# A hybrid Mamba and attention block on one core: other start steps for the front and gate parts, and one convolution moved from TensorE to VectorE

## The chip, the core and the metric

The kernel runs on one core of a Trainium2 chip. A core has five engines with instruction queues of their own: TensorE (in the profile PE, its weight loads PEld), VectorE (DVE), ScalarE (ACT), GpSimd (POOL) and SyncE (SP). They meet only through semaphores. Data moves between the chip's memory and the core by DMA; here SP issues the plain transfers and POOL the accumulating ones, which add what they carry to what stands at the target. The metric is the time of one execution in microseconds, and smaller is better. A profile is one further execution, recorded by the hardware.

## The reference

The input is 8 images of 256 channels and 32 x 32 positions, taken as 8 batches of 1024 tokens, all in fp32. Layer 0 is a Mamba block and a feed-forward network; layer 1 is an attention block and a mixture of experts. Cut to what matters:

```python
# layer 0: the Mamba block
xm, z = split(layernorm(x) @ W_in)                     # 512 inner channels each
xm = silu(sum(pad(xm)[:, k:k+L] * conv_w[:, k] for k in range(4)) + conv_b)
dt, Bm, Cm = split(xm @ W_x)                           # 16 states
dt = softplus(dt @ W_dt + b_dt)
h  = exp(dt_t * A) * h + (dt_t * x_t) * B_t            # for each token t, 512 channels x 16 states
y  = sum_over_states(h * C_t) + xm * D_param
x  = x + (y * silu(z)) @ W_out
x  = x + gelu(layernorm(x) @ W1 + b1) @ W2 + b2
# layer 1
t  = t + softmax(q @ k.T / sqrt(32) + column_bias) @ v @ Wo + bo        # q, k, v of layernorm(t), 8 heads
t  = t + layernorm(xt + top-2-of-8 experts(xt))                         # xt = layernorm(t), routed per batch
```

The recurrence over the tokens has to run in their order. A batch's attention needs all its 1024 tokens, and its experts need its attention.

## The kernel before

**Chunks and steps.** The work is cut into 16 chunks of 512 tokens (`CH`). Chunk i is one half of batch i // 2: even chunks are first halves, odd ones second halves, which carry on the state of the half before. A chunk has 32 steps (`NSTEP`): 16 states for each of two halves of the 512 inner channels. A step handles one state for 256 channels, laid out as 128 partitions x 2 x 512 tokens. For each step (`now` in the main loop at the end of `hybrid_kernel`):

- `scan`: VectorE runs the recurrence over `hb` (one 128x1024 scan in even chunks, two of 128x512 in odd ones, which start from `state`). In even chunks POOL copies the last column of `hb` to `state`.
- `decay`: ScalarE computes `exp(dt * A)` into `da_all`, for the step after next. `da_all` has two buffers, so the decay of step n + 2 waits for the scan of step n.
- `inputs`: VectorE forms `hb = xm * bc` for the next step; `bc` holds a state's B and C rows on all partitions, loaded by SP.
- `sums`: VectorE multiplies `hb` by the C row, and POOL issues a DMA that adds `hb` into `dx`, the block's output y.

These are VectorE's 3 or 4 instructions per step, and the next step's follow directly.

**Everything else is laid between the steps.** It is written as generators that emit a few instructions and yield. `start(stream, key)` puts one into a list, and `advance()`, called several times per step, lets those that are due emit. The order of a queue is thus settled when the program is built, by a planner: `Model` and `Queue` keep an estimated time for each engine by the cost functions (`vec_cost`, `act_cost`, `pe_cost`, `pool_cost`), a stream goes on when its own last work is over by these estimates, and `URGENT` ranks the streams (attention, then prologue, gate and epilogue, then projection and experts); those of lower rank hold back when TensorE's or ScalarE's queue is more than `LAG` ahead. Where TensorE would have nothing to do, `keep_warm` emits filler matmuls, in the profile `warm<-mean_c,zero_c`, or adds zeros to a sum that is open. The emission happens in one helper, so nearly all instructions have line L100 in the profile, and DMAs L95; tiles are told by name. The streams:

- `prologue(i + 1)`, the front part of the next chunk. It loads `xn` (SP), normalises it, stores it as `xn_d` (SP), multiplies by `w_in`, convolves, applies Silu, multiplies by `w_x`, brings the B and C rows to memory (SP), computes `dt` by softplus, and multiplies `xm` by `dt`. The softplus is put together in `dt` by two or three accumulating DMAs (`add`, tiles `e` and `u`) that POOL issues for each half; `SOFT[i]` picks one of two ways of computing its parts. The last step, `xm<-xm,dt` on VectorE, waits for the last of these to land. It starts at step `FRONT[i]` of chunk i (at step 1 where the list says less).
- The convolution inside it has two forms, chosen by `CONV[i]`. `conv_dve` takes the first tap on ScalarE (`xm<-xp,vecs`, 4 per chunk) and the other three on VectorE (`xm<-xp,vecs,xm`, 12 `scalar_tensor_tensor` of 128x512). `conv_pe` takes all taps on TensorE with 32x32 diagonal tiles, 64 matmuls `xin<-xp,taps`, and copies the result out on ScalarE (`xm<-xin,vecs`, 4).
- `gate_part(i)` computes Silu(z): a load of `xn_d` (SP), eight matmuls `z`, four copies out and two Silu on ScalarE, for which its function table is changed before and after. It starts at step `GATE[i]` of chunk i and is needed in the epilogue.
- `epilogue(i)` starts at the last step: the product with the gate, the multiplication by `w_out`, the layer norm, the feed-forward network with its Gelu, and the layer norm that gives layer 1's input (`tn_t`).
- `attention(b)` (scores `sc`, exponentials `pt`, sums `num` and `den`), `project_part(b, c, ..)` and `experts(b)` (`xe`, `he`, `re`, with gathers of the weights that POOL issues) follow once both chunks of a batch are through. The last batch's come after the last step and make up the tail.

Before the next chunk's first steps the main loop lets time pass, in the plan, until that chunk's `dt` is there:

```python
if i + 1 < B * NCH and k == max(FRONT[i], 1):
    start(prologue(i + 1), ("p", i + 1), model.t)
if k == GATE[i]:
    start(gate_part(i), ("g", i), model.t)
...
while "dt" not in chunk.get((now + 2) // NSTEP, {}):
    idle(0.5)
```

Of the kernel before, what the change touches and what calls it, by code (L numbers as in the profile page):

```python
# [54 lines left out]
def hybrid_kernel(ctx: ExitStack, tc: tile.TileContext, a: dict, out: bass.AP):  # L55
# [204 lines left out]
    T4, H4, PT, AHEAD, LAG, TICK = 25, 4, 4, 2, 8.0, 0.15  # L260


    FRONT = (8, 1, 6, 2, 6, 9, 6, 3, 12, 2, 13, 3, 7, 5, 7)
    GATE = (10, 16, 17, 17, 17, 17, 12, 12, 17, 14, 20, 16, 24, 21, 17, 17)
    CONV = (0, 0, 1, 1, 0, 0, 0, 0, 0, 0, 0, 0, 0, 1, 0, 0)
    SOFT = (0, 0, 1, 1, 1, 1, 0, 0, 0, 0, 0, 0, 0, 0, 0, 0)


# [288 lines left out]
    def prologue(i: int):  # L557
# [11 lines left out]

        xm = yield from (conv_pe if CONV[i] else conv_dve)(i, xn, mem)  # L570
        mem.put(xn, at=max(stored, model.end))
# [239 lines left out]
    def gate_part(i):  # L811

        while not set_up:
            yield POLL
        me = chunk[i]
        mem = Owner(t4, 3, 2)
        xn = yield from mem.take(f"xz_{i}")
        yield sp.dma_start(xn, me["xn_d"])
        sz, ps = [], None
        for d in range(ND + 1):  # L820
            if d:
                h, q = divmod(d - 1, 2)
                act.activation(
                    sz[h][:, q, :], ps, AF.Identity, bias=b_in[:, ND + d - 1 : ND + d]
                )
                banks.put(ps)
            if d < ND:
                if d % 2 == 0:
                    sz.append((yield from mem.take(f"sz_{i}_{d // 2}")))
                ps = yield from banks.take(f"z_{i}_{d}")  # L830
                for k in range(KC):
                    pe.matmul(
                        ps, w_in[:, k, DI + d * P : DI + (d + 1) * P], xn[:, k, :],
                        start=(k == 0), stop=(k == KC - 1),
                    )
                yield
        mem.put(xn)
        for t in sz:
            act.activation(t, t, AF.Silu)
        lnexp()  # L840
        mem.end()
        yield
        me["sz"] = sz
# [916 lines left out]
    with tc.tile_pool(name="work", bufs=1) as work_pool:  # L1760
# [30 lines left out]
        def start(stream, key, at=0.0):  # L1791
            due.append([at, URGENT[key[0]], len(done) + len(due), stream, key])
# [120 lines left out]
        for now in range(nsteps):  # L1913
            i, k = divmod(now, NSTEP)
# [4 lines that stand above are left out]
# [295 lines left out]
```

## Time and profile before

| | us |
|---|---|
| median of 8 runs | 3561.09 (3552.91 to 3564.25) |
| the profiled execution | 3554.77 |
| its span | 3553.0 |
| VectorE busy | 3062.1 |
| TensorE busy, fillers included | 3229.8 |
| of that, the fillers `warm` | 409.6 |
| ScalarE busy | 2470.6 |
| from the last `hb` to the end (tail) | 418.2 |

The profiled execution lies 6.3 us below the median. A chunk is told in the trace by its `hb` instructions: chunk 0 runs from 70.0 to 307.4 us of the span, chunk 15 from 2973.8 to 3134.8, and the others take 170 to 209 us each. Before chunk 0 stand 70 us of set-up and of the first prologue. In a list of waits each line names the waiting engine and tile, what released it, the total, how often, and the longest. In a timeline each row has start, duration, engine, line, operation, output and operands, and in brackets the idle time in front of it with its releaser. In a row of windows the clock of TensorE is a share of full speed.

### The profile page before, as it was taken

What the parts mean: (1) busy time and instruction counts of PE and PEld (TensorE: products, weight loads), DVE (VectorE), ACT (ScalarE), POOL (GpSimd) and SP (SyncE); (2) the same over time, 40 slices, a digit from 0 to 9 for tenths busy, and PEclk for the clock granted to TensorE, in tenths of its full rate; (3) what the DMA queues carried; (4) which work ended last, traced back from release to release, by engine and by line L of the source; (5) the groups of instructions that cost most, each with busy time, mean ns of one, the idle gap of its engine ahead of it and who ended that gap; (6) DMA issues with size and microseconds to landing.
All of it is one profiled execution on the core that took longest, in us unless ns stands there. A gap on an engine that the chain in (4) does not pass through costs nothing.

```text
span 3553.0 us, 40220 instructions
## 1 busy us (share of the span) xinstructions
PE 3229.8 (91%) x14535; PEld 1404.0 (40%) x14535; DVE 3062.1 (86%) x3148; ACT 2470.6 (70%) x3563; POOL 937.8 (26%) x1058
## 2 busy tenths in 40 slices
PE   8767879998999898999999999999999999999997
PEld 5544344333433334333443334333433334334344
DVE  6979999899999798999999899989998999943551
ACT  5553737695778766787778867887788776864644
POOL 0232223222332123322332233223432332211010
PEclk9878989998999998999999999999999999999999
DMA  4756978787799778898787987799888878942120
GB/s 121 196 128 158 202 171 190 171 185 176 177 216 213 159 177 185 201 197 204 188 199 177 204 193 183 185 202 205 209 201 188 196 181 192 207 108 69 38 75 15
DMA packets 189504, 607.80 MB, mean 171 GB/s; under 512 B 27056, under 2 KB 38000, under 8 KB 189296
## 3 DMA queue, kind: packets, MB, share of 16 engines
q0 software_dynamic: 103968, 366.54, 53.3%
q1 hardware_dynamic: 85328, 238.60, 20.8%
q8 instruction: 116, 1.90, 0.2%
q14 instruction: 92, 0.75, 0.1%
HBM read 238.58 MB, written 62.39 MB: 85 GB/s over the span
## 4 chain that ended last, share of the span: by engine, by line
PE 22%; DVE 16%; ACT 5%; issue 4%; DMA 2%; POOL 1%; DVEq 0%; POOLq 0%; ACTq 0%
DVE hb L100 12%; PE num L100 3%; PE sc L100 2%; PE re L100 2%; PE facc L100 2%; PE he L100 2%; PE den L100 1%; PE fh L100 1%; PE warm L100 1%; PE halves L100 1%; ACT L100 1%; POOL state L100 1%; PE z L100 1%; ACT da_all L100 1%; DMA dt<-u 1%
## 5 line engine op out<-in xcount | busy, mean ns | idle before, releaser
L100 ACT ACTIVATE da_all<-dt,vecs 128x512 f32<-128x512 f32 (+1 forms) x1024 | 701.3, 717 | 442.8 <-DVE hb L100 439.6
L95 POOL DMA_DIRECT2D dx<-hb x512 | 444.5, 871 | 1669.3 <-DVE hb L100 1367.9
L100 DVE TENSOR_TENSOR hb<-hb,bc 128x1024 f32<-128x1024 f32 x512 | 624.8, 1220 | 37.3 <-POOL state L100 27.0
L100 DVE TENSOR_TENSOR_SCAN hb<-da_all,state,hb 128x512 f32<-128x512 f32 x512 | 631.5, 1268 | 7.7 <-ACT da_all L100 7.6
L100 DVE TENSOR_TENSOR hb<-xm,bc 128x1024 f32<-128x1024 f32 x512 | 618.2, 1207 | 7.9 <-DMA dx<-hb 7.7
L100 DVE TENSOR_TENSOR_SCAN hb<-da_all,hb 128x1024 f32<-128x1024 f32 x256 | 584.4, 2283 | 2.7 <-ACT da_all L100 2.7
L100 ACT ACTIVATE pt<-sc 128x1024 f32<-128x1024 f32 x512 | 494.1, 1017 | 92.5 <-PE sc L100 81.9
L100 PE MATMUL warm<-mean_c,zero_c 128*128 128x256 f32 x1368 | 409.6, 428 | 35.2 <-ACT dt L100 9.7
L100 PEld LDWEIGHTS warm<-mean_c,zero_c 128*128 128x128 f32 x1368 | 259.1, 206 | 200.3 <-PE warm L100 81.4
L100 PE MATMUL sc<-qk,qk 32*128 32x512 f32 x2048 | 324.8, 645 | 11.2 <-ACT pt L100 10.6
L100 PE MATMUL num<-pt,v 128*32 128x512 f32 x2048 | 281.1, 620 | 44.5 <-DVE ot L100 44.5
L100 POOL COPY state<-hb 128x2 f32<-128x2 f32 x256 | 209.5, 818 | 367.4 <-DVE hb L100 350.0
L100 PE MATMUL den<-pt,ecb 128*32 128x512 f32 x1792 | 243.8, 615 | 0.0
L100 PE MATMUL facc<-fh,w 128*128 128x512 f32 x512 | 231.4, 598 | 3.9 <-DVE xf_x L100 1.8
L100 PE MATMUL fh<-x_f,w 128*128 128x512 f32 x480 | 230.4, 610 | 4.2 <-DVE x_f L100 1.7
L100 PE MATMUL he<-xe,g 128*128 128x512 f32 x448 | 218.3, 612 | 3.1 <-DVE x_f L100 1.8
L100 ACT ACT_TABLE_LOAD x169 | 216.8, 1283 | 3.5 <-PEq L2201 0.7
L100 PE MATMUL re<-he,g 128*128 128x512 f32 x472 | 213.8, 596 | 2.3 <-DVE xn L100 2.2
L100 PEld LDWEIGHTS sc<-qk,qk 32*128 32x128 f32 x2048 | 95.8, 185 | 183.5 <-issue 76.1
L100 PE MATMUL mo<-sz,w_out 128*128 128x512 f32 x256 | 125.0, 633 | 25.5 <-DVE sz L100 24.3
L100 PEld LDWEIGHTS facc<-fh,w 128*128 128x128 f32 x512 | 94.6, 190 | 130.8 <-issue 120.7
L100 PEld LDWEIGHTS fh<-x_f,w 128*128 128x128 f32 x480 | 87.9, 192 | 131.3 <-issue 109.5
(364 smaller groups left out, 4286.9 us busy)
## 6 DMA issues: line engine op xcount, KB each, us to landing
dx<-hb POOLq DMA_DIRECT2D x512, 512.0 KB, 6.6
bc<-bc_d SPq DMA_DIRECT2D x256, 512.0 KB, 4.6
dt<-e POOLq DMA_DIRECT2D x38, 512.0 KB, 8.5
dt<-u POOLq DMA_DIRECT2D x30, 512.0 KB, 9.0
xe<-xf_d SPq DMA_DIRECT2D x28, 512.0 KB, 6.6
xn<-in_x SPq DMA_DIRECT2D x16, 512.0 KB, 6.4
xn_d<-xn SPq DMA_DIRECT2D x16, 512.0 KB, 4.8
xz<-xn_d SPq DMA_DIRECT2D x16, 512.0 KB, 7.4
```

What stands on the lines that cost most here:

```text
L95: f(*args, **kw)
L100: return f(*args, **kw)
```

## The change

Three lists are edited, which hold one entry per chunk. Nothing else in the source differs.

```diff
-    FRONT = (8, 1, 6, 2, 6, 9, 6, 3, 12, 2, 13, 3, 7, 5, 7)
-    GATE = (10, 16, 17, 17, 17, 17, 12, 12, 17, 14, 20, 16, 24, 21, 17, 17)
-    CONV = (0, 0, 1, 1, 0, 0, 0, 0, 0, 0, 0, 0, 0, 1, 0, 0)
+    FRONT = (5, 3, 5, 2, 6, 10, 6, 2, 12, 3, 13, 3, 7, 5, 10)
+    GATE = (10, 16, 17, 17, 17, 23, 12, 18, 17, 14, 20, 23, 24, 21, 17, 24)
+    CONV = (0, 0, 1, 0, 0, 0, 0, 0, 0, 0, 0, 0, 0, 1, 0, 0)
     SOFT = (0, 0, 1, 1, 1, 1, 0, 0, 0, 0, 0, 0, 0, 0, 0, 0)
```

- `FRONT` differs in seven of its 15 entries: chunk 0: 8 to 5, 1: 1 to 3, 2: 6 to 5, 5: 9 to 10, 7: 3 to 2, 9: 2 to 3, 14: 7 to 10. Entry i is the step of chunk i at which the prologue of chunk i + 1 begins.
- `GATE` differs in four of 16: chunk 5: 17 to 23, 7: 12 to 18, 11: 16 to 23, 15: 17 to 24.
- `CONV[3]` goes from 1 to 0: the convolution of chunk 3, which is done during chunk 2, is taken by `conv_dve` instead of `conv_pe`. Chunks 2 and 13 stay with `conv_pe`.

Since the planner settles each queue's order with all streams together, a moved start also shifts other streams around it. In the built program the order of the instructions is the same as before in chunks 6 and 10 to 13 (the new `GATE[11]` moves nothing), nearly the same in 4 and 9, and different in 0, 1, 2, 3, 5, 7, 8, 14, 15 and the tail. TensorE has 64 matmuls for the convolution less and nine fillers more; VectorE has the 12 `xm<-xp,vecs,xm` more; ScalarE has one table load less.

## The prediction

> **What bounds the kernel now.** I read the page first, then the time of each chunk window by window, then what VectorE waits for in the chunks that the change touches, and last the order of the work around those waits. The profiled execution took 3554.77 us, 6.3 below the median of 3561.09; all durations are its own, and the sum is made against it and carried over to the median. A measurement of this kernel tells about 0.2% (7.1 us) from no change.
>
> The page: span, engines, and the chain of work that ended last.
> ```profile
> span 3553.0 us, 40220 instructions
> PE 3229.8 (91%) x14535; PEld 1404.0 (40%) x14535; DVE 3062.1 (86%) x3148; ACT 2470.6 (70%) x3563; POOL 937.8 (26%) x1058
> DVE hb L100 12%; PE num L100 3%; PE sc L100 2%; PE re L100 2%; PE facc L100 2%; PE he L100 2%; PE den L100 1%; PE fh L100 1%; PE warm L100 1%; PE halves L100 1%; ACT L100 1%; POOL state L100 1%; PE z L100 1%; ACT da_all L100 1%; DMA dt<-u 1%
> ```
> TensorE looks fullest, but part of that is fillers (`warm`), and the heaviest single entry of the chain is VectorE's `hb`. Windows by chunk settle it (start:end, length, then busy time per engine, clock, DMA share, GB/s); here chunks 2, 3, 5, 7, 15 and the tail:
> ```profile
> 477.40:657.00 179.60, 155.90 (x608) 70.97 (x608) 160.08 (x115) 107.72 (x157) 65.12 (x72) 0.91 0.81 179
> 657.00:845.80 188.80, 175.36 (x910) 62.48 (x908) 178.84 (x174) 150.99 (x211) 35.44 (x41) 0.95 0.79 179
> 1039.30:1248.10 208.80, 190.52 (x942) 73.03 (x946) 185.98 (x184) 164.22 (x233) 39.94 (x46) 0.95 0.79 179
> 1441.00:1619.80 178.80, 167.71 (x789) 65.76 (x788) 176.99 (x169) 150.54 (x214) 47.78 (x50) 0.97 0.90 206
> 2973.80:3134.80 161.00, 156.67 (x715) 59.41 (x717) 160.63 (x149) 129.43 (x173) 41.88 (x44) 1.00 0.91 205
> 3134.80:3553.00 418.20, 386.74 (x1846) 167.01 (x1838) 152.76 (x298) 212.70 (x268) 32.85 (x35) 0.98 0.20 53
> ```
> Chunks 7 and 15 are VectorE end to end (177.0 of 178.8, 160.6 of 161.0 us). A chunk's length is VectorE's work plus its waits: chunk 2 waits 19.5 us and chunk 5 22.8. The tail is TensorE (387 of 418). So inside the chunks the change is priced in VectorE work and VectorE waits; in the tail in TensorE work.
>
> What VectorE waits for in chunk 2 (total, times, longest):
> ```profile
> DVE xm L100 <- ACT pt L100: 8.3, 1, 8.3
> DVE xm L100 <- DMA dt<-e: 4.1, 1, 4.1
> DVE tn_t L100 <- PE var_t L100: 2.4, 1, 2.4
> ```
> and in chunk 5:
> ```profile
> DVE xm L100 <- ACT dx L100: 12.9, 1, 12.9
> DVE tn_t L100 <- PE mu_t L100: 4.0, 1, 4.0
> ```
> The ScalarE names are not the true releaser: `xm<-xm,dt` needs the accumulating DMAs that POOL issues into `dt`. POOL's timeline at the end of chunk 2, and VectorE's two multiplications behind it:
> ```profile
> 631.73 0.86 POOL L95 DMA_DIRECT2D dt<-e  x1
> ...
> 637.49 0.85 POOL L95 DMA_DIRECT2D dt<-e  x1 [3.29 <-DMA dt<-u]
> ```
> ```profile
> 641.35 1.23 DVE L100 TENSOR_TENSOR xm<-xm,dt 128x1024 f32<-128x1024 f32 x1 [8.30 <-ACT pt L100]
> 646.66 1.23 DVE L100 TENSOR_TENSOR xm<-xm,dt 128x1024 f32<-128x1024 f32 x1 [4.08 <-DMA dt<-e]
> ```
> Issue to use is 9.6 and 9.2 us, as the page's table of DMA issues has it (median us last):
> ```profile
> dt<-e POOLq DMA_DIRECT2D x38, 512.0 KB, 8.5
> dt<-u POOLq DMA_DIRECT2D x30, 512.0 KB, 9.0
> ```
>
> **The change part by part.**
>
> *Convolution of chunk 3 (done during chunk 2).* 64 tap matmuls leave TensorE and 12 `scalar_tensor_tensor` come to VectorE. Their rows (min/median/max ns):
> ```profile
> L100 DVE SCALAR_TENSOR_TENSOR xm<-xp,vecs,xm x156: 723/751/753, 25.9 to 2873.1; 128x512 f32<-128x512 f32 x156
> L100 PE MATMUL xin<-xp,taps x384: 585/587/612, 344.1 to 2512.7; 32*32 32x512 f32 x192
> ```
> VectorE: 12 x 0.751 = +9.0 us (8.0 if they start every 0.67, as packed pairs do). I take **+9.0**, since nothing covers VectorE's work. TensorE loses four bursts of 3.64 = 14.6 us, worth nothing in itself beside a fuller VectorE. ScalarE's four copies out cost 0.812 instead of 0.668: +0.6, covered, since it is busy 108 of 180 us.
>
> *Prologue 3 earlier* (`FRONT[2]` 6 to 5, and the shorter TensorE queue). Its last additions into `dt` move from step 29 to steps 23 and 26; between them and the multiplications VectorE now has 17.1 and 11.8 us of work, before 1.2 each. With 8.5 to 9.0 to landing both waits go: 8.3 + 4.1 = **-12.4** (bounds: -12.4, and 0 if something else is late then). The multiplication of `tn_t` has 3.5 us of VectorE work ahead of it instead of 1.2, so its wait goes by **-2.3**. What is late next in this chunk is `x_f` on TensorE's mean, 1.7, unchanged.
>
> *Chunk 5.* `FRONT[5]` 9 to 10 starts prologue 6 a step later, yet `GATE[5]` 17 to 23 takes gate work from ahead of it, so the last additions stay at step 29. VectorE work from the last exponential's subtraction to the multiplication rises from 3.0 to 6.2 us: the 12.9 wait shrinks by **-3.2** (bounds -3.2 and 0, if the chain itself moves back as much).
>
> *Other fronts.* 0: 8 to 5, 1: 1 to 3, 7: 3 to 2, 9: 2 to 3, 14: 7 to 10. Each moves, on SP, the load of `xn`, the store of `xn_d` and the row loads behind them; on POOL, two or four additions into `dt` among the `dx` additions. The work between the last addition and its use becomes 9.0 (for chunk 1), 8.2 (chunk 9) and 9.4 (chunk 15) us; before, 9.4 for chunk 9 left no wait. Against 9.0 to landing that is 0 to +2 together; **+0.5**. In chunk 0 the Silu pair of gate 0 (2 x 1.05) leaves the set-up chain, which waits 13.3 us in four pieces for ScalarE (`b_norm`): **-2.0** (bounds 0, and -7.4 for a whole gate group). Six gathers on POOL move off the state copies of chunk 14 (a 3.2 us wait to about 0.7) and nearer those of chunk 8 (+1): **-1.5**; the rows of such waits run from 0 to 4.7, so bounds -4 and +4.
>
> *Late decays.* ScalarE's exponentials `da_all` have two buffers; scans wait 10.3 us for them in the whole run. In the new order 10 to 13 us of ScalarE work stands in front of a decay at three new places (chunk 1, steps 19 and 23; chunk 7, step 30); four such places of the trace waited 2.5, 1.6, 0.9 and 0.4, mean 1.35. 3 x 1.35 less a 0.8 that goes: **+3.2** (bounds 0 and +7.5).
>
> *Gates.* `GATE` 5: 17 to 23, 7: 12 to 18, 15: 17 to 24; 11: 16 to 23 changes no order. Each group is eight `z` matmuls, four copies of 0.68, two Silu of 1.05 and two table loads of 1.283: 7.4 us of ScalarE. In chunk 5 (ScalarE's timeline, two rows of the four)
> ```profile
> 1188.60 1.28 ACT L100 ACT_TABLE_LOAD   x1
> 1189.89 2.01 ACT L100 ACTIVATE sz<-sz 128x1024 f32<-128x1024 f32 x2
> ```
> the loads and Silus ran from 1188.60 to 1193.21 and VectorE waited for no decay in that chunk, so I price them at 0 beyond the above; the cover is ScalarE's 10 to 45 idle us per chunk.
>
> *Tail.* Four more of attention 6's units of exponentials finish before the last step, so 11.6 us of TensorE leaves the tail; eight expert matmuls and a filler come in. Real TensorE work falls 297.1 to 291.5 (-5.7), but up to the first row of attention 7 it grows by 5.6. Nearer to the mix of both: **-1.2** (bounds -6 and +5.6).
>
> Sum: 9.0 - 12.4 - 2.3 - 3.2 + 0.5 - 2.0 - 1.5 + 3.2 - 1.2 = -9.9. On the profiled run 3544.9, on the median **3551**.
>
> **The rivals.**
>
> *1. The wait comes back elsewhere.* Chunk 2 gets 9.0 us more VectorE work, and its 12.4 us of waits move to another late input, the next in line being the first decays and `bc` rows of chunk 3. For it: 19.5 us of waits in a chunk with TensorE at 156 of 180. Against: the cover of 11.8 us exceeds the landing time. It gives -9.9 + 12.4 = +2.5: 3563.6, no change.
>
> *2. ScalarE's queue makes it slower.* The gate groups of chunks 5, 7 and 15 now stand among the last steps, where the softplus of the next chunk, the feed-forward's Gelus and the decays need the same queue. Exposed in full, 3 x 7.4 = 22.2: -9.9 + 22.2 = +12.3, 3573. Slower is reached when more than 17 us of it shows. For it: chunk 5's ScalarE is the fullest (164 of 209) and the wait there is already on this chain. Against: no row so far shows a gate group waited for.
> The Trainium skill, "ScalarE: Activation LUTs", section "What ACT_TABLE_LOAD costs", puts a drain of some 1.38 us behind each load's 1.283, which as an estimate would make a group 10.2 and the three 30 us. This trace doesn't agree so far: the load at 1188.60 takes 1.28 and the Silu starts at 1189.89; by the trace the sum stays as above.
>
> *3. The tail keeps its backlog.* Gate 15's last copies and Silus (4.6 us with their loads) end after the last step, and TensorE's extra 5.6 is not won back: +10.2 instead of -1.2, so +1.5, 3562.6. For it: TensorE runs without a gap from 3134 to 3223. Against: the attention work then left over is shorter.
>
> **How the numbers follow.** Forecast 0.58; 0.06 of that lies within 0.2%, where terms come out near their dear ends. Rival 1 0.08 and rival 3 0.08, both within 0.2%; rival 2 0.26, slower. So faster 0.52, same 0.22, slower 0.26. All cheap ends together give 8.0 - 12.4 - 2.3 - 3.2 - 7.4 - 4 - 6 = -27.3, 3534, too much luck at once; from 3538, to 3573, where half of rival 2 is left out.
>
> **What would show it.** Right: chunk 2 no longer than before (about 174 us) with VectorE at 169 busy and no wait of `xm` on `dt<-e`; chunk 5 near 205; chunks 0 and 1 within 3 us; the tail 412 to 424. Wrong: waits of `hb` on `da_all` above 20 us in all, or a new `xm` wait in chunks 7, 8 or 14 (rival 2); chunk 2 above 180 (rival 1); the span after the last `hb` above 425 (rival 3).

## The result and the profile after

The changed kernel took 3544.14 us in the median of 14 runs (3532.94 to 3553.78), against 3560.46 of 39 runs before: a ratio of 0.9952, with a 95% interval of 0.9943 to 0.9962, or 16 to 17 us less. A second measurement, among the experiments below, gave 0.9937 (0.9921 to 0.9954). The forecast was 3551, faster. The profiled execution has a span of 3542.1 us, 10.9 below that of before, so the two profiles show only a part of what the medians show.

The page of the changed kernel, its first two lines:
```profile
span 3542.1 us, 39995 instructions
PE 3225.5 (91%) x14425; PEld 1405.3 (40%) x14425; DVE 3069.9 (87%) x3160; ACT 2469.9 (70%) x3562; POOL 934.0 (26%) x1058
```
VectorE is busy 7.8 us longer, and the kernel shorter all the same: what went is waiting. The windows of chunks 2, 3, 5, 7 and 15 and the tail (start:end, length, busy time per engine, clock, DMA share, GB/s); as before the change, the tail is counted from the end of the last `hb` of the steps:
```profile
473.70:649.30 175.60, 148.45 (x500) 72.25 (x498) 168.61 (x127) 107.23 (x155) 63.96 (x72) 0.94 0.82 183
649.30:832.50 183.20, 170.59 (x920) 62.54 (x920) 178.81 (x174) 150.44 (x211) 35.70 (x41) 0.98 0.82 184
1024.80:1226.00 201.20, 194.26 (x954) 76.03 (x958) 185.95 (x184) 164.71 (x233) 39.84 (x46) 0.97 0.82 186
1418.00:1603.10 185.10, 164.85 (x764) 62.29 (x764) 175.08 (x166) 148.25 (x208) 50.20 (x49) 0.96 0.87 195
2968.00:3131.10 163.10, 159.79 (x759) 57.20 (x759) 162.03 (x152) 130.19 (x175) 41.31 (x43) 0.99 0.89 206
3131.10:3542.10 411.00, 378.20 (x1746) 168.08 (x1745) 151.40 (x294) 206.22 (x263) 33.52 (x36) 0.98 0.20 52
```
Chunk 2 has 168.6 us of VectorE work instead of 160.1 and is still 4.0 shorter; chunk 5 has the same work and is 7.6 shorter; the tail is 7.2 shorter with 8.5 less of TensorE. Chunk 7 is 6.3 longer with 1.9 less work.

What VectorE waits for in chunk 2, the three longest entries:
```profile
DVE x_f L100 <- PE mu_f L100: 1.6, 1, 1.6
DVE tn_t L100 <- PE mu_t L100: 1.5, 1, 1.5
DVE tn_t L100 <- PE var_t L100: 1.1, 1, 1.1
```
and in chunk 5, the four longest:
```profile
DVE tn_t L100 <- PE var_t L100: 4.0, 1, 4.0
DVE r L100 <- ACT r L100: 3.9, 2, 3.0
DVE xm L100 <- ACT dx L100: 3.0, 1, 3.0
DVE xm L100 <- DMA dt<-u: 1.5, 1, 1.5
```
The 8.3 and 4.1 of `xm` in chunk 2 are gone as forecast. The 12.9 of chunk 5 has become 3.0 + 1.5, a good deal more than the 3.2 that I had allowed.

The name on the 12.9 is partly true. `dx<-xm,vecs` on ScalarE reads the tile that `xm<-xm,dt` writes over, so the first multiplication has to wait for it as well as for `dt`. Three rows of before: the addition `u` for this half (issued at 1213.48; the last figure is the time to its landing), ScalarE's `dx`, and the multiplication:
```profile
dt<-u POOLq DMA_DIRECT2D x1, 512.0 KB, 13.1
1229.17 2.55 ACT L100 ACTIVATE dx<-xm,vecs 128x512 f32<-128x512 f32 x4
1230.54 1.23 DVE L100 TENSOR_TENSOR xm<-xm,dt 128x1024 f32<-128x1024 f32 x1 [12.95 <-ACT dx L100]
```
and the same three after (`u` issued at 1193.90):
```profile
dt<-u POOLq DMA_DIRECT2D x1, 512.0 KB, 9.5
1205.24 2.55 ACT L100 ACTIVATE dx<-xm,vecs 128x512 f32<-128x512 f32 x4
1206.61 1.23 DVE L100 TENSOR_TENSOR xm<-xm,dt 128x1024 f32<-128x1024 f32 x1 [3.03 <-ACT dx L100]
```
Before, VectorE was free at 1217.6 and `u` landed at 1226.5: some 9.0 us of the wait are the landing, and the last 4.0 are the first two of the four `dx`, which ended at 1230.51. After, `u` landed at 1203.4, just before VectorE was free, and the 3.0 is `dx` alone. In all nine profiles with the new order of chunk 5 this wait is 3.0 us and ends with the second `dx`.

One wait of VectorE's has grown. It is that for a free `hb` buffer, which needs the addition of an older `hb` into `dx` to have landed. The page's group of `inputs`, before and then after:
```profile
L100 DVE TENSOR_TENSOR hb<-xm,bc 128x1024 f32<-128x1024 f32 x512 | 618.2, 1207 | 7.9 <-DMA dx<-hb 7.7
```
```profile
L100 DVE TENSOR_TENSOR hb<-xm,bc 128x1024 f32<-128x1024 f32 x512 | 618.5, 1208 | 14.2 <-DMA dx<-hb 14.2
```
The two groups of scans went from 7.7 + 2.7 to 7.0 + 4.6 us of idle time in front of them: +1.2.

**By chunk, over all profiles.** In the built programs the change falls into parts that don't touch each other: `FRONT[0]` and `FRONT[1]` order chunks 0 and 1; `FRONT[2]` with `CONV[3]` chunks 2 to 4; `FRONT[5]` with `GATE[5]` chunk 5; `GATE[7]` chunks 7 and 8 (with 12 there, both have the order of before even where `FRONT[7]` is 2, so `FRONT[7]` moves nothing); `FRONT[14]` chunk 14 and with `GATE[15]` chunk 15 and the tail. So every profile of this study gives, for each chunk, one more sample of the old order or of the new one. The means (in brackets the spread and the number of profiles), worked out from the start of each chunk's first scan and, for the tail, from the end of the last `hb`:

| place | order of before, us | order of after, us | difference | forecast |
|---|---|---|---|---|
| chunk 0 | 239.2 (237.4-240.2, 7) | 235.7 (235.2-236.1, 7) | -3.5 | -2.0 |
| chunk 1 | 169.8 (169.3-170.6, 7) | 168.4 (167.9-169.3, 7) | -1.3 | +1.9 |
| chunk 2 | 179.5 (178.3-181.4, 5) | 176.2 (174.6-178.2, 7) | -3.2 | -5.7 |
| chunks 3 and 4 | 379.4 (377.7-382.2, 5) | 375.1 (373.5-376.4, 7) | -4.2 | 0 |
| chunk 5 | 209.9 (208.9-211.0, 4) | 201.1 (200.5-201.6, 9) | -8.8 | -3.2 |
| chunk 7 | 182.4 (178.8-185.1, 7) | 184.5 (180.7-185.7, 6) | +2.1 | +1.4 |
| chunk 8 | 195.0 (193.1-196.9, 7) | 199.2 (196.8-200.6, 6) | +4.2 | +1.0 |
| chunk 14 | 194.3 (193.2-195.6, 4) | 198.0 (194.8-200.9, 9) | +3.7 | -2.5 |
| chunk 15 | 161.4 (161.0-162.2, 4) | 163.0 (162.5-164.0, 8) | +1.7 | 0 |
| tail | 417.8 (417.2-418.4, 4) | 411.6 (410.2-412.5, 8) | -6.2 | -1.2 |

The differences of the table, unrounded, come to -15.7 us, about what the medians show.

### The profile page after: what moved, and what is told of

Its sections match the earlier page's. It is cut to its first block, busy times and chain, and to the rows that moved or that the text cites. A ratio compares the mean times of both kernels' runs of the same rounds, so it can differ in the third digit from the quotient of the medians.

```text
span 3542.1 us, 39995 instructions
## 1 busy us (share of the span) xinstructions
PE 3225.5 (91%) x14425; PEld 1405.3 (40%) x14425; DVE 3069.9 (87%) x3160; ACT 2469.9 (70%) x3562; POOL 934.0 (26%) x1058
## 5 line engine op out<-in xcount | busy, mean ns | idle before, releaser
L100 DVE TENSOR_TENSOR hb<-hb,bc 128x1024 f32<-128x1024 f32 x512 | 624.7, 1220 | 36.7 <-POOL state L100 26.3
L100 POOL COPY state<-hb 128x2 f32<-128x2 f32 x256 | 200.6, 784 | 364.5 <-DVE hb L100 348.7
```

The lines of the kernel that those rows point to most:

```text
L100: return f(*args, **kw)
```

## The experiments

The theory: the gain is VectorE waits taken away, place by place, and the places add up. The rivals: the gain sits in the tail alone; the convolution's move is what makes chunk 2 early; the later gates cost, or do nothing.

**Chunks 2 to 4 alone.**
```diff
-    FRONT = (8, 1, 6, 2, 6, 9, 6, 3, 12, 2, 13, 3, 7, 5, 7)
-    CONV = (0, 0, 1, 1, 0, 0, 0, 0, 0, 0, 0, 0, 0, 1, 0, 0)
+    FRONT = (8, 1, 5, 2, 6, 9, 6, 3, 12, 2, 13, 3, 7, 5, 7)
+    CONV = (0, 0, 1, 0, 0, 0, 0, 0, 0, 0, 0, 0, 0, 1, 0, 0)
```


> The kernel before with FRONT[2] = 5 and CONV[3] = 0 alone, which gives chunks 2 to 4 the order of the changed kernel and all others the order of before. My forecast's terms for this part: +9.0 of VectorE work, -12.4 and -2.3 of waits, so -5.7 us, a ratio of 0.9984, with chunk 2 near 174 and chunk 3 as before. What the two profiles show side by side goes further: chunks 2, 3 and 4 are shorter by 4.1, 5.5 and 1.2 us, so -10.8 and 0.9970, if the gain in chunk 3 belongs to this part too. The rival that the waits come back elsewhere: 0 to +2.5, 1.000 or above.

Measured: 0.9967 (0.9955 to 0.9979), about -12. Its windows of chunks 2 and 3:
```profile
479.30:653.90 174.60, 151.47 (x496) 72.90 (x496) 168.66 (x128) 107.11 (x155) 65.06 (x72) 0.91 0.82 184
653.90:836.70 182.80, 171.25 (x920) 62.16 (x920) 178.66 (x174) 149.99 (x211) 35.49 (x41) 0.97 0.82 185
```
So the gain in chunk 3, which the forecast had at nothing, belongs to this part: chunk 3 came to 182.8, as in the changed kernel, with everything outside chunks 2 to 4 ordered as before. In all five profiles with the old order VectorE's rows show 2.4 to 3.3 us in front of `hb_120` (step 24 of the chunk) for a landing of `dx` and 2.5 in front of `hb_113` for a decay. With the new order the first is gone, with at most 1.7 in front of a later `hb`, and the second is 1.9 or less. The rival that the waits come back elsewhere falls.

**Chunk 5 alone.**
```diff
-    FRONT = (8, 1, 6, 2, 6, 9, 6, 3, 12, 2, 13, 3, 7, 5, 7)
-    GATE = (10, 16, 17, 17, 17, 17, 12, 12, 17, 14, 20, 16, 24, 21, 17, 17)
+    FRONT = (8, 1, 6, 2, 6, 10, 6, 3, 12, 2, 13, 3, 7, 5, 7)
+    GATE = (10, 16, 17, 17, 17, 23, 12, 12, 17, 14, 20, 16, 24, 21, 17, 17)
```


> The kernel before with FRONT[5] = 10 and GATE[5] = 23 alone; only chunk 5 gets another order. My forecast: -3.2 us (0.9991). The profiles side by side: chunk 5 went from 208.9 to 201.2, so -7.7 (0.9978). The ScalarE rival: a gate group of 7.4 us in front of the softplus or the decays, up to +7.4 less 3.2 = +4.2 (1.0012).

Measured: 0.9975 (0.9963 to 0.9988), about -9, with chunk 5 at 200.9. The side-by-side reading holds, the forecast's 3.2 doesn't.

**The gate of chunk 5 alone.**
```diff
-    GATE = (10, 16, 17, 17, 17, 17, 12, 12, 17, 14, 20, 16, 24, 21, 17, 17)
+    GATE = (10, 16, 17, 17, 17, 23, 12, 12, 17, 14, 20, 16, 24, 21, 17, 17)
```


> The kernel before with GATE[5] = 23 alone and FRONT[5] = 9 as before; chunk 5 gets an order of its own, and the planner then orders all later chunks anew, so that only chunk 5 is to be read. In the trace of before the gate's loads and Silus (1188.6 to 1193.2 us) stand directly in front of the softplus of chunk 6 on ScalarE. If that was the cause of the 12.9 us wait, chunk 5 goes from 208.9 to 201 or less, since the prologue also starts a step earlier than in the changed kernel. If FRONT[5] = 10 is what helped, chunk 5 stays at 208 to 211.

Measured: chunk 5 at 202.4, and in its waits `xm` has only 0.5 us left. Its window of chunk 5, and that wait:
```profile
1035.90:1238.30 202.40, 194.63 (x982) 74.11 (x982) 185.22 (x183) 167.34 (x236) 39.19 (x45) 0.97 0.82 185
```
```profile
DVE xm L100 <- DMA dt<-u: 0.5, 1, 0.5
```
It was the gate, through all that it moves in the chunk's order (ScalarE's `dx` too now came in time). The whole kernel was slower, 1.0068 (1.0051 to 1.0086): a start step that no other entry answers to gives all later chunks another order (chunk 7 took 201.5, chunk 8 210.8). What the gate stood in front of is seen on ScalarE. Before:
```profile
1188.60 1.28 ACT L100 ACT_TABLE_LOAD   x1
1189.89 2.01 ACT L100 ACTIVATE sz<-sz 128x1024 f32<-128x1024 f32 x2
1191.91 1.28 ACT L100 ACT_TABLE_LOAD   x1
1193.21 0.69 ACT L100 ACTIVATE e<-v,vecs 128x512 f32<-128x512 f32 x1
```
and after:
```profile
1167.59 0.69 ACT L100 ACTIVATE e<-v,vecs 128x512 f32<-128x512 f32 x1
...
1180.37 1.28 ACT L100 ACT_TABLE_LOAD   x1
1181.66 2.00 ACT L100 ACTIVATE sz<-sz 128x1024 f32<-128x1024 f32 x2
1183.67 1.28 ACT L100 ACT_TABLE_LOAD   x1
1184.97 0.69 ACT L100 ACTIVATE e<-v,vecs 128x512 f32<-128x512 f32 x1
```
`e<-v`, two for each half, begins the next chunk's softplus, and with it the chain to the awaited `dt`. Before, the group of loads and Silus stood between the first half's two (at 1182.54 and 1193.21); after, both of the first half are through (the second at 1167.59), and only the second half's stand behind the group. Counted from a scan on VectorE, the first half's `e` was subtracted 11.4 us after the first scan of step 26 before (1186.3 to 1197.7), and 1.2 us after it now (1172.0 to 1173.2). POOL issues the first half's `u`, for which the multiplication waits, right behind the second half's `e`: 27.2 us after that scan before, and 21.9 now. It landed 40.3 and 31.5 us after the scan. So of 8.8 us gained 5.3 are the earlier chain and 3.5 the quicker landing (13.1 and 9.5 us from issue); what made the landing quicker no run shows.

**Chunks 7 and 8 alone.**
```diff
-    FRONT = (8, 1, 6, 2, 6, 9, 6, 3, 12, 2, 13, 3, 7, 5, 7)
-    GATE = (10, 16, 17, 17, 17, 17, 12, 12, 17, 14, 20, 16, 24, 21, 17, 17)
+    FRONT = (8, 1, 6, 2, 6, 9, 6, 2, 12, 2, 13, 3, 7, 5, 7)
+    GATE = (10, 16, 17, 17, 17, 17, 12, 18, 17, 14, 20, 16, 24, 21, 17, 17)
```


> The kernel before with FRONT[7] = 2 and GATE[7] = 18 alone; chunks 7 and 8 get the order of the changed kernel. My forecast: one late decay at +1.4 and +1 from the gathers, so about +2.4 us (1.0007). The profiles side by side: chunk 7 +6.3 and chunk 8 +3.7, +10.0 (1.0028), with the new waits of hb on the landing of dx in chunk 7. If those waits are the chance of one execution, about 0.

Measured: 1.0009 (0.9999 to 1.0018), +3. By this time alone that is not told from nothing; that the later gate of chunk 7 costs is read from the chunks of all profiles and from the pair of runs without it below. A new wait stands at step 26 in all six profiles with the new order (3.0 to 3.7 us in front of `hb_251`) and in none of seven with the old one. The changed kernel's POOL queue in front of it, and then VectorE's row:
```profile
1554.61 0.86 POOL L95 DMA_DIRECT2D dx<-hb  x1 [5.28 <-DVE e L100]
1555.15 1.20 POOL L95 DMA_DIRECT2D dt<-e  x1
1555.69 1.55 POOL L95 DMA_DIRECT2D dt<-u  x1
1557.72 0.86 POOL L95 DMA_DIRECT2D re<-xf_d  x1 [0.49 <-DMA re<-y_d]
1561.29 0.86 POOL L95 DMA_DIRECT2D dx<-hb  x1 [2.71 <-DMA dx<-hb]
1564.65 0.86 POOL L95 DMA_DIRECT2D dx<-hb  x1 [2.51 <-DVE hb L100]
1567.63 0.86 POOL L95 DMA_DIRECT2D dt<-u  x1 [2.12 <-ACT da_all L100]
1575.90 0.86 POOL L95 DMA_DIRECT2D dx<-hb  x1 [7.41 <-DMA dx<-hb]
```
```profile
1575.39 1.22 DVE L100 TENSOR_TENSOR hb<-xm,bc 128x1024 f32<-128x1024 f32 x1 [3.23 <-DMA dx<-hb]
```
`hb_251` takes the buffer of `hb_247`, whose addition is the one issued at 1561.29; its use at 1575.39 comes 14.1 us later, against 6.6 from issue to landing in the page's median. Three additions into `dt` and a transfer into `re` were issued among three into `dx` from 1554.6 to 1567.6. That these crowd it out is argued from the order; no run took one of them away.

**Chunks 14, 15 and the tail alone.**
```diff
-    FRONT = (8, 1, 6, 2, 6, 9, 6, 3, 12, 2, 13, 3, 7, 5, 7)
-    GATE = (10, 16, 17, 17, 17, 17, 12, 12, 17, 14, 20, 16, 24, 21, 17, 17)
+    FRONT = (8, 1, 6, 2, 6, 9, 6, 3, 12, 2, 13, 3, 7, 5, 10)
+    GATE = (10, 16, 17, 17, 17, 17, 12, 12, 17, 14, 20, 16, 24, 21, 17, 24)
```


> The kernel before with FRONT[14] = 10 and GATE[15] = 24 alone; chunks 14, 15 and the tail get the order of the changed kernel. My forecast: -2.5 for the gathers, up to +0.5 for the shorter cover of dt, -1.2 in the tail: about -3 us (0.9991). The profiles side by side: chunk 14 +5.2, chunk 15 +3.4, tail -8.6: 0 (1.0000). If the tail keeps a backlog (my third rival): the tail +10 longer, 1.003.

Measured: 0.9983 (0.9975 to 0.9992), -6, with the tail at 411.6, chunk 15 at 163.0 and chunk 14 at 200.5 (the expectation's +3.4 and -8.6 draw the line between chunk 15 and the tail 1.3 us later, behind a wait). The rival of a backlog in the tail falls. Its profile alone would say 0; chunk 14 is why the two differ: in the new order it took 194.8 to 195.0 in four profiles and 200.2 to 200.9 in five, with nothing between. The granted clock of TensorE goes with the two levels, as the last section shows.

**Which of the two makes the tail.**
```diff
-    GATE = (10, 16, 17, 17, 17, 23, 12, 18, 17, 14, 20, 23, 24, 21, 17, 24)
+    GATE = (10, 16, 17, 17, 17, 23, 12, 18, 17, 14, 20, 23, 24, 21, 17, 17)
```


> The changed kernel with GATE[15] = 17 of before and FRONT[14] = 10 kept; chunk 14 keeps the new order, chunk 15 and the tail get one of their own. If it is the later gate of chunk 15 that lets attention 6 go ahead of it on TensorE and ScalarE before the last step, the tail goes back from 410.6 to about 418 and chunk 15 from 164.2 to 161: 4.3 us slower than the changed kernel, 0.9964. If FRONT[14] did it, the tail stays at 410 to 412 and the ratio at 0.9952 or below.

Measured: 0.9958 (0.9943 to 0.9972), beside the changed kernel's 0.9937 (0.9921 to 0.9954) on the same chip. Chunk 15 and the tail:
```profile
2970.40:3132.40 162.00, 158.27 (x762) 55.64 (x764) 160.46 (x150) 126.98 (x171) 41.30 (x43) 0.99 0.89 207
3132.40:3546.50 414.10, 382.19 (x1756) 170.98 (x1748) 152.61 (x297) 208.81 (x266) 33.49 (x36) 0.98 0.19 52
```
With the old gate the tail is 414.1, between the means of the table (417.8 and 411.6). The expectation's 410 to 412 and 418 count it from VectorE's next instruction after the last `hb`, which here leaves out 2.4 us of waiting and gives 411.7. Chunk 15 and the tail together don't depend on where the line is drawn: 576.2 here, against 579.2 in the mean of the old order and 574.7 of the new one (573.2 to 576.4). So the later front of chunk 14 makes the larger part, about 3.0 of the 4.5 us. Whether the gate of chunk 15 makes the rest stays open: the sum lies within the spread of the new order, and the ratio lies between the two readings (0.9952 and 0.9964) and 0.0021 above that of the changed kernel, with overlapping intervals.

**The new steps, with the convolution of chunk 3 on TensorE.**
```diff
-    CONV = (0, 0, 1, 0, 0, 0, 0, 0, 0, 0, 0, 0, 0, 1, 0, 0)
+    CONV = (0, 0, 1, 1, 0, 0, 0, 0, 0, 0, 0, 0, 0, 1, 0, 0)
```


> The changed kernel with CONV[3] = 1, so all new start steps, with the convolution of chunk 3 on TensorE as before; only chunk 2 differs from the changed kernel. VectorE has 9.0 us less to do there, but the last additions into dt of chunk 3 come at steps 28 and 29 with 7.1 and 1.2 us of VectorE work before their use, against 9.6 and 9.2 from issue to use: waits of about 2.5 and 6 to 8, and the 2.4 of tn_t. My theory (the prologue's start and the work behind the additions decide): chunk 2 near 175 to 178, the whole within 2 us of the changed kernel. Rival (it was the load on TensorE that made chunk 2 late, and the step does nothing): waits of 12.4 stay, chunk 2 at 179 to 181, 0.9965. Rival (the convolution's VectorE work is a dead loss): 9 us faster than the changed kernel, 0.9927.

Measured: 0.9958 (0.9943 to 0.9973). Chunk 2, its window and its wait:
```profile
472.60:647.30 174.70, 149.34 (x587) 66.65 (x585) 160.36 (x115) 105.62 (x155) 68.24 (x72) 0.95 0.84 184
```
```profile
DVE xm L100 <- DMA dt<-e: 10.6, 2, 7.5
```
Of VectorE's 8 us less work, all is given back as a wait of 10.6 for `dt`. So the convolution's place is worth next to nothing here: it trades work for wait, and by the chunk's length the start of the prologue is what gains. It doesn't gain by the wait for `dt`, of which the five profiles of the old order have 12.2 to 12.4 and the two of this order 10.6 and 10.2; the other waits of the chunk went from 5.9 to 8.6 us down to 3.7 and 3.8. Both other readings (chunk 2 at 179 to 181; 9 us faster) fall, the first by the chunk alone, since its ratio of 0.9965 lies in the interval. No run moves the convolution without the start step.

**The whole without chunks 0 and 1.**
```diff
-    FRONT = (5, 3, 5, 2, 6, 10, 6, 2, 12, 3, 13, 3, 7, 5, 10)
+    FRONT = (8, 1, 5, 2, 6, 10, 6, 2, 12, 3, 13, 3, 7, 5, 10)
```


> The changed kernel with FRONT[0] = 8 and FRONT[1] = 1 of before; chunks 0 and 1 get the order of before again. My forecast for that part was -2.0 + 1.9 + 0.2, about 0, so 0.9952 again. The four parts run alone came to -11.7 - 8.9 + 3.2 - 6.0 = -23.4 against -17.1 for the whole; if they add up, chunks 0 and 1 cost 6.3 and this run shows 0.9934. The profiles say the opposite: chunk 0 took 237.4 to 240.2 in five profiles with the order of before and 235.4 in the changed kernel, so this run would be 3.6 slower than the changed kernel, 0.9962.

Measured: 0.9947 (0.9934 to 0.9960), the same as the whole within its interval. It decides little by its time: 0.9934 and 0.9952 lie in the interval, and 0.9962 just outside; by its profile chunk 0 took 240.0, and the seven profiles a side put chunk 0 at -3.5.

**The whole without chunks 7 and 8, twice, and the whole again.**
```diff
-    FRONT = (5, 3, 5, 2, 6, 10, 6, 2, 12, 3, 13, 3, 7, 5, 10)
-    GATE = (10, 16, 17, 17, 17, 23, 12, 18, 17, 14, 20, 23, 24, 21, 17, 24)
+    FRONT = (5, 3, 5, 2, 6, 10, 6, 3, 12, 3, 13, 3, 7, 5, 10)
+    GATE = (10, 16, 17, 17, 17, 23, 12, 12, 17, 14, 20, 23, 24, 21, 17, 24)
```


> The changed kernel with FRONT[7] = 3 and GATE[7] = 12 of before; chunks 7 and 8 get the order of before again. If the parts add up, this is the changed kernel without the +3.2 us that its part of chunks 7 and 8 cost alone (1.0009): -17.1 - 3.2 = -20.3, a ratio of 0.9943. If the two profiles told it rightly (+10.0 in these chunks), 0.9924. If the waits on the landing of dx in chunk 7 come in any order (they did, at 4.5 and 4.8, in two runs whose chunk 7 has the order of before), 0.9950, as the changed kernel.

Measured: 0.9941 (0.9928 to 0.9953), which fits the sum of the parts, excludes 0.9924 and leaves 0.9950 open. Beside the changed kernel on one chip:

> The changed kernel once more, beside the three below on the same chip: 0.9952 as before.

> The changed kernel with FRONT[7] = 3 and GATE[7] = 12 of before, once more. By the chunks of ten profiles the new order costs 1.7 us in chunk 7 (a wait of 3.0 to 3.4 us at step 26 in all four profiles with that order, none in the others) and 3.5 in chunk 8: 5.2 less than the changed kernel, a ratio of 0.9937 against its 0.9952. If the parts of chunks 7 and 8 are as good in either order: 0.9952 for both.

Measured: 0.9937 (0.9921 to 0.9954) for the changed kernel and 0.9921 (0.9906 to 0.9936) without the part of chunks 7 and 8; medians 3538.76 (3530.26 to 3542.82) and 3531.62 us (3528.35 to 3536.41). The intervals overlap, yet both times the version without that part was ahead, and the table's two rows come to 6.3 us. It is the fastest version of this study, and faster than both kernels as far as six runs each can tell.

**The same with the convolution back on TensorE.**
```diff
-    FRONT = (5, 3, 5, 2, 6, 10, 6, 2, 12, 3, 13, 3, 7, 5, 10)
-    GATE = (10, 16, 17, 17, 17, 23, 12, 18, 17, 14, 20, 23, 24, 21, 17, 24)
-    CONV = (0, 0, 1, 0, 0, 0, 0, 0, 0, 0, 0, 0, 0, 1, 0, 0)
+    FRONT = (5, 3, 5, 2, 6, 10, 6, 3, 12, 3, 13, 3, 7, 5, 10)
+    GATE = (10, 16, 17, 17, 17, 23, 12, 12, 17, 14, 20, 23, 24, 21, 17, 24)
+    CONV = (0, 0, 1, 1, 0, 0, 0, 0, 0, 0, 0, 0, 0, 1, 0, 0)
```


> As the run before, and with CONV[3] = 1, the convolution of chunk 3 on TensorE. My theory now is that the convolution's place is worth nothing either way: 9.0 us of VectorE work against 10.5 of waits in chunk 2, so the same ratio as its neighbour, 0.9937, within 0.0005. If the convolution on VectorE is a loss where the rest is better: 0.9912.

Measured: 0.9950 (0.9933 to 0.9968), not the 0.9937 within 0.0005 that I expected, and 0.0029 above its neighbour, with overlapping intervals. Its six times fall into two groups, 3531.66 and 3532.61 and then 3540.99 to 3545.97 us, and the profile is of the first. Its profiled execution has a span of 3530.8, its neighbour's 3531.1; chunk 2 took 174.5, against 176.2 in the mean of seven with the convolution on VectorE. Medians and chunks point opposite ways, so whether the convolution is worth a few us on one side stays open; a loss of 9 is excluded.

## Why the prediction was right

The direction and the range were right, and the waits of the largest term went as forecast. Point by point, by its own steps:

- *Convolution and prologue 3.* +9.0 of work came as +8.5 busy, the waits of 12.4 went whole, chunk 2 came out 3.2 shorter instead of 5.7. But the two terms are not apart: with the start step and no convolution on VectorE 10 of the 12.4 stay, so most of the wait went because the convolution's own work now fills it. The step that was off is the 2.3 for `tn_t`: waits of `tn_t` on TensorE's means and variances were 2.4 + 1.1 in chunk 2 and are still 1.5 + 1.1. That the clearance of 11.8 us would cover the landing was right.
- *Chunks 3 and 4* had no term at all; they gave 4.2. The order of chunk 3 moves too: POOL issues the last addition into `dt` 142 us into the chunk instead of 130, and the wait for a landing of `dx` at step 24 is gone. I had looked only for what would be late next in chunk 2.
- *Chunk 5* was the mis-sized term, -3.2 against -8.8. I counted the VectorE work behind the last subtraction and missed that the chain itself starts earlier. The step that failed is "VectorE waited for no decay in that chunk, so I price them at 0": nobody waited for a decay, but the wait of 12.9 was the end of a chain that went through ScalarE directly behind the two table loads, as the row at 1193.21 showed. "The ScalarE names are not the true releaser" failed there too: it holds in chunk 2, where the awaited addition landed at 641.26 and the multiplication started at 641.35, but in chunk 5 ScalarE's `dx` ended the wait, 4.0 us after the landing.
- *Rival 2* had the sign of this the wrong way round in chunk 5, and right in chunks 7 and 8, though not by ScalarE: there a later gate costs 6.3 in waits that include those on `dx`, while some 1.8 of VectorE work slides from chunk 7 to 8.
- *Late decays* were +1.2 over the run instead of +3.2, and not where I had put them: the three places that I named waited 0.3 us in all in the changed kernel (1.5 in its second profile), and 3.3 (3.4) stand in front of the last scan of chunk 14, which I had not listed. *Set-up* in chunk 0 was -3.5 instead of -2.0. *Gathers*: the wait for `state` was 27.0 before and 26.3 after, -0.7 instead of -1.5.
- *Tail.* -6.2 against -1.2, just outside the bound of -6; in the profile it is 411.0, below the 412 to 424 that I had named as a sign. TensorE's time there fell by 8.5. Of the backlog of 5.6 that I had set against the 5.7 of work only 2.1 came: the first exponential of attention 7 stands 134.4 us behind the last `hb` instead of 132.2, and the start of its last `ot` on VectorE 289.1 instead of 294.8, 5.7 us earlier. The bound that the work gave was the better value. Against it stand +1.7 in chunk 15 and +3.7 in chunk 14, for which I had 0 and -2.5. VectorE's layer norm of 1.4 us that slides from the tail into chunk 15 makes most of the first; the late decay is part of the second.
- *Rival 3* falls with the tail, *rival 1* with the chunks 2 to 4 alone.
- *The rule on table loads* (the Trainium skill, "ScalarE: Activation LUTs", section "What ACT_TABLE_LOAD costs", some 1.38 us of drain behind each load): in the rows above the next instruction starts 1.29 to 1.30 us after each load's start, before and after. Two loads and two Silus held the queue for 4.6 us; no row shows the drain.

So the sum was right in sign and 6 us short, the errors in chunk 5, chunks 3 and 4 and the tail (-15) being larger than those on the other side in chunks 7, 8, 14 and 15 (+12), with smaller ones between. That errors of this size leave no more than 6 us is luck; the direction rests on the waits in chunks 2 and 5, which did go.

## What to carry to other kernels

A wait is priced from the start of the chain that it ends, engine by engine, not only from the work behind the chain's last link: work on a second engine that "nobody waits for" can stand in front of the first link, as the gate's 4.6 us stood in the softplus here. A releaser's name that looks false is held against the time of the landing: the wait may end twice, as in chunk 5, first with the DMA and then with a reader of the tile. Moving work off the bounding engine gained next to nothing in chunk 2, where the next input of that engine came no earlier; nearly the same 9 us were first work and then wait. And where a change splits into parts that leave each other's order alone, each part can be run by itself, and each profile is a sample of every part: the samples of all profiles together corrected what two profiles side by side had wrong by up to 4 us.

## What was not expected of the hardware

Chunks with the same order of instructions don't repeat equally well. Chunk 13 took 195.9 or 196.0 us in eleven of thirteen profiles, and the tail in its new order repeats within 2.3; chunk 11, whose order none of these kernels changes, took 189.4 to 190.7 in five and 193.3 to 193.7 in eight. The granted clock of TensorE goes with the two levels: it is 0.98 or 0.99 over the chunk in the five and 0.96 in the eight. In each of the eight it is at half for one stretch of 10.2 us, some 142 us into the chunk, and in the five for 3.4 us there or not at all. Chunk 14 in its new order shows the same: the five profiles at 200.2 to 200.9 us have a stretch of 10.2 to 13.7 us at half clock that begins 131 to 135 us into the chunk, and the four at 194.8 to 195.0 have none there. That stretch in the changed kernel (200.8), and the same place in the run with the convolution on TensorE (194.8); the figure after the five engines is the clock:
```profile
2898.80:2912.50 13.70, 12.70 (x43) 6.94 (x44) 9.98 (x13) 8.13 (x16) 2.09 (x4) 0.50 0.55 130
2894.40:2908.10 13.70, 12.56 (x69) 8.52 (x69) 13.47 (x18) 9.33 (x17) 2.94 (x5) 1.00 0.75 180
```
TensorE has 43 matmuls in the one and 69 in the other. In its old order chunk 14 took 195.4 and 195.6 us at a clock of 0.94 over the chunk and 193.2 and 193.3 at 0.96 to 0.97, so like with like the new order costs about 5 us at the low clock and 1.6 at the high one. No run set the clock, so that it makes the levels is argued, and what lowers it there is open.

In chunk 7 a wait of 4.5 to 5.0 us for a landing of `dx` stood at step 4 in nine profiles of thirteen, in either order. So a chunk's single pair of profiles can show 4 us or more that no edit made, as it did in chunks 7, 11 and 14 here.
